# Five edits to the setup of a gated cross-attention kernel: mem read in rows of 128 features, four staging buffers, x transposed earlier, gate's bias added by DMAs

## The chip, the cores and the metric

The kernel runs on one core of a Trainium2 chip. The metric is the device time of one execution in microseconds (us). Before the change it is 984.94 us, the median of three runs (984.9 to 985.8).

## What is computed

Everything is float32. x is (8, 1024, 1024), the context ("mem") is (8, 64, 512). For each of the 8 batches:

```python
mp   = mem @ W_mem.T                      # (64, 1024)
attn = softmax(x @ mp.T / 32)             # (1024, 64)
ctx  = attn @ mp                          # (1024, 1024)
gate = sigmoid(concat(x, ctx) @ W_gate.T + b_gate)
f    = x + gate * ctx
out  = f / sqrt(mean(f*f) + 1e-6) * norm_w
```

The kernel doesn't form ctx before it goes into gate. Since a row of attn adds up to 1, ctx @ W2.T + b_gate is attn @ (mp @ W2.T + b_gate), where W2 is the half of W_gate that meets ctx. So the setup computes mp and "mg" = mp @ W2.T (+ b_gate) once for all 512 rows of mem, and stores both in device memory (`mpd`, mp transposed; `mgd[0]`, mp; `mgd[1]`, mg). The main loop loads 64 rows of each per batch into one tile `mg`: mp in partitions 0 to 63 and mg in partitions 64 to 127.

## The kernel before

**The setup.** mem is loaded as two tiles `memq` (128 rows by 2 by 512), TensorE transposes it in 16 pieces of 128 by 128 (`transpose_mem`, L189), and VectorE and ScalarE copy the pieces from PSUM to `memT`. `chunks` (L107) picks the features of chunk k as every fourth float of a row; w_mem is loaded to match, with four neighbouring rows in one partition (`rows_by_chunk`, L103). Then 32 products `pm` give mp transposed (L213), copied to four tiles `mpT` (m11 to m22). mg is one Strassen step (Winograd's form): seven products `pg` in the order 1, 6, 5, 2, 7, 4, 3 (`mg_product`, L435), summed into c11, c12, c21, c22 by VectorE (`mg_sum`, L450), with gate's bias added by GpSimd (`mg_bias`, L454), and stored to `mgd[1]` (`store_mg`, L459). `store_mp` (L413) has VectorE transpose a quarter of mp into a staging tile `mpq` and stores it to `mgd[0]` by four DMAs; the staging tiles are two buffers, named `it2` and `it3`.

**The main loop.** x comes in 16 parts q of 512 rows, two per batch. x @ W1.T is a two-level Strassen product: seven outer products per q, in the order 1, 6, 7, 5, 4, 2, 3 (`ORDER`, L537), each of seven inner products A, B, C, D, A, E, F (`outer_product`, L683). An inner product is a "slot"; a q has 49. `plan` (L540) puts the other engines' work of a q at slots by hand: `inner_s` (GpSimd, the sums `l` of the left side), `outer_s`, the scores `psT` (slot 7), softmax, the transposed attention `attnT`, the context products `pc` (in outer products 5, 4, 2, 3), `transpose_x` of the next q and so on. The right side's sums are made once: `outer_sum` (L224, tiles t5, t6, t4) and `inner_sum` (L227, tiles it1 to it7, four sums of 128 by 512 for each outer product). Those of 1 are made on VectorE and of 7 and 6 on GpSimd in the setup; those of 5, 4, 2, 3 are spread by L575 over slots 3 to 23 of q=0, on VectorE.

**What sets the order.** `pin` keeps each engine's instructions in the order in which the program writes them, so each engine and each DMA queue is a list worked off from the front; an instruction that waits holds up what stands behind it on its engine. The tile framework adds the waits. Three kinds matter here. A tile with a tag takes a buffer of that tag's pool and waits until its last user is done: `mp_l`, c21 and the `l` tiles share the two buffers of tag `l2`; x of the first q takes the buffer of w_mem (tag `xq`). Plain DMAs all go out on SP's queue (`load`, L97), and each takes the next of eight lanes, so it waits for the DMA eight places ahead of it. The accumulating DMA of the residual (L600) goes out on GpSimd's queue.

**The order around the change** (L465 to L524): sums s1, s2, t7; s3 and the sums of 7 on GpSimd; product 1; store_mp(2), (3); product 6; store_mp(0); product 5 with c12's bias; store_mp(1); t6; load_mp(0); product 2 with c11's bias; w2's sums and t4; GpSimd's sums of 6; product 7; x's transposes and l of product 1; product 4 with c21's bias; x's other transposes; product 3; load_mg(0); then the main loop.

Of the kernel before, what the change touches and what calls it, by code (L numbers as in the profile page):

```python
# [8 lines left out]
F32 = mybir.dt.float32  # L9
AF = mybir.ActivationFunctionType  # L10
ALU = mybir.AluOpType
# [4 lines left out]
P = 128  # L16
# [4 lines left out]
def tile_gated_cross_attention_rmsnorm(  # L21
# [72 lines left out]
    def tt(eng, o, a, b, op):  # L94
        pin(eng.tensor_tensor(o, a, b, op))  # L95

    def load(o, i):  # L97
        pin(nc.sync.dma_start(o, i))

    def t4k(pool, shape, tag, name):  # L100
        return pool.tile(shape, F32, tag=tag, name=name)

    def rows_by_chunk(w, n):  # L103

        return w.rearrange("(p j) f -> p j f", j=n)

    def chunks(t, n):  # L107

        return t.rearrange("p s e -> p (s e)").rearrange("p (m j) -> p j m", j=n)
# [14 lines left out]
    memr = mem.rearrange("b m e -> (b m) e").rearrange("(g s p) e -> g p s e", g=2, p=P)  # L124
    memq = [t4k(rot, [P, 2, E], "l2", f"memq{i}") for i in range(2)]
    wm = t4k(xqpool, [P, KE, D], "xq", "wm")
    wmr = rows_by_chunk(w_mem_t, KE)
    pin(nc.scalar.dma_start(wm[:, 0, :], wmr[:, 0, :]))
    for g in range(2):
        load(memq[g], memr[g])  # L130
# [11 lines left out]
    w1 = [const.tile([P, 4, D], F32, name=f"w1_{h}") for h in range(2)]  # L142
    for h in range(2):
        load(w1[h], rows_by_chunk(w_gate_t[:D, :], KD)[:, 4 * h : 4 * h + 4, :])
    bias_sb = t4k(small, [P, D], "junk", "bias_sb")
    load(bias_sb, b_gate.partition_broadcast(P))
    nw_sb = const.tile([P, D], F32, name="nw_sb")
    load(nw_sb, norm_w.partition_broadcast(P))
    xq = {}
# [1 line left out]
    def load_xq(q):  # L151
        b, n0 = q // QPB, (q % QPB) * QT
        xq[q] = t4k(xqpool, [P, 16, Q4], "xq", f"xq{q}")
        src = x[b, n0 : n0 + QT, :].rearrange("(s c) (i e) -> i c s e", c=32, i=4)
        for i in range(4):
            load(xq[q][32 * i : 32 * (i + 1), :, :], src[i])
# [32 lines left out]
    def transpose_mem(g):  # L189

        cols = slice(g * (BM // 2), (g + 1) * (BM // 2))
        for k in range(KE):
            for r in range(2):
                n = 2 * g + r
                pin(
                    nc.tensor.transpose(
                        pt[k][:, n * P : (n + 1) * P],
                        chunks(memq[g][:, r : r + 1, :], KE)[:, k],
                        ident,
                    )  # L200
                )
            o = memT[k // 2][:, k % 2, cols]
            pin((nc.scalar.copy if k % 2 else nc.vector.tensor_copy)(o, pt[k][:, cols]))
# [23 lines left out]
    def inner_sum(eng, o, n):  # L227
        s, a, b = ((T1, R12, R11), (T2, R22, T1), (R12, R22, R12), (T4, R21, T2))[n]
        tt(eng, w_op(o, s), w_op(o, a), w_op(o, b), ALU.subtract)
# [13 lines left out]
    def transpose_x(q, t, half):  # L243

        key = q, t // 2, half
        if key not in A:
            A[key] = t4k(
                apool, [P, KH, 2 * P], f"a{t // 2 + 1}{half + 1}", f"a{t // 2 + 1}{half + 1}_{q}"
            )
        r = t % 2  # L250
        pin(
            nc.vector.transpose(  # L252
                A[key][:, :, r * P : (r + 1) * P],
                chunks(xq[q][:, 4 * t : 4 * t + 4, :], KD)[:, half * KH : (half + 1) * KH],
            )
        )
# [30 lines left out]
    def inner_s(q, o, part):  # L287
        l11, l12, l21, l22 = quarters(left(q, o))
        if part == 0:
            L2[q, o] = t4k(rot, [P, 4, 2, P], "l2", f"l2_{q}_{o}")  # L290
        s1, s2, s3, s4 = (L2[q, o][:, i, :, :] for i in range(4))
        if part == 0:
            tt(nc.gpsimd, s1, l21, l22, ALU.add)
            tt(nc.gpsimd, s2, s1, l11, ALU.subtract)
        else:
            tt(nc.gpsimd, s3, l11, l21, ALU.subtract)
            tt(nc.gpsimd, s4, l12, s2, ALU.subtract)
# [68 lines left out]
    def load_mp(b):  # L366
        mps[b] = t4k(small, [P, KD, M], "mpb", f"mpb{b}")
        load(mps[b], mpd[:, :, b * M : (b + 1) * M])

    def load_mg(b):  # L370
        mgs[b] = t4k(small, [P, D], "mg", f"mg{b}")
        for g in range(2):
            load(mgs[b][g * M : (g + 1) * M, :], mgd[g, b * M : (b + 1) * M, :])

    KH = KD // 2
# [22 lines left out]
        for r, copy in ((0, nc.vector.tensor_copy), (1, nc.scalar.copy)):  # L400
            pin(copy(mpT[r][j // KH][:, j % KH, :], pm[j][:, r * HM : (r + 1) * HM]))
    (m11, m12), (m21, m22) = mpT
    load_xq(0)
    for r in range(2):
        for h in range(2):
            load(mpd[:, h * KH : (h + 1) * KH, r * HM : (r + 1) * HM], mpT[r][h])

    def mp_step(eng, tag, pool, a, b, op):
        t = t4k(pool, [P, KH, HM], tag, f"mp_{tag}")
# [3 lines left out]
    def store_mp(g):  # L413

        r, n = g // 2, g % 2
        mpq = const.tile([P, 4, Q4], F32, tag=f"it{2 + n}", name=f"mpq{g}")
        for h in range(2):
            pin(
                nc.vector.transpose(
                    chunks(mpq, KD)[:, h * KH : (h + 1) * KH],  # L420
                    mpT[r][h][:, :, n * P : (n + 1) * P],
                )
            )
        for i in range(4):
            load(
                mgd[0, g * P : (g + 1) * P, i * Q4 : (i + 1) * Q4].rearrange(
                    "(s c) e -> c s e", c=32
                ),
                mpq[32 * i : 32 * (i + 1), :, :],
            )  # L430
# [4 lines left out]
    def mg_product(n, l, r):  # L435
        nonlocal mg_next
        pgs = []
        for t in range(2):
            tag = mg_banks[mg_next % 8]
            mg_next += 1  # L440
            pg = (ps_ctx if tag == "ctx" else ps).tile([P, H], F32, tag=tag, name=f"pg{n}_{t}")
            for k in range(KH):
                mm(pg, l[:, k, t * P : (t + 1) * P], r[k], k == 0, k == KH - 1)
            pgs.append(pg)
        return pgs
# [5 lines left out]
        for t in range(2):  # L451
            tt(nc.vector, o[:, t, :], a[:, t, :], pgs[t], ALU.add)

    def mg_bias(eng, o, h):  # L454
        b = bias_sb[:, h * H : (h + 1) * H]
        for t in range(2):
            tt(eng, o[:, t, :], o[:, t, :], b, ALU.add)

    def store_mg(o, r, h):  # L459
        load(  # L460
            mgd[1, r * HM : (r + 1) * HM, h * H : (h + 1) * H].rearrange("(t p) e -> p t e", p=P),
# [14 lines left out]
    pgs = mg_product(1, m11, b11)  # L476
    for t in range(2):
        pin(nc.scalar.copy(c11[:, t, :], pgs[t]))
    store_mp(2)
    store_mp(3)  # L480
    pgs = mg_product(6, s2, t2)
    mg_sum(c21, c11, pgs)
    store_mp(0)
    tt(nc.gpsimd, s2, m12, s2, ALU.subtract)
    pgs = mg_product(5, s1, t1)
    mg_sum(c12, c21, pgs)
    mg_bias(nc.gpsimd, c12, 1)
    store_mp(1)
    w1_place(6)
    outer_sum(6, 3, 5)  # L490
    load_mp(0)
    pgs = mg_product(2, m12, b21)
    mg_sum(c11, c11, pgs)
    mg_bias(nc.gpsimd, c11, 0)
    store_mg(c11, 0, 0)
    w2_sum(nc.vector, b21, b21, t2)
    w1_place(4)
    outer_sum(4, 2, 6)
    for n in range(4):
        inner_sum(nc.gpsimd, 6, n)  # L500
    pgs = mg_product(7, s3, b12)
    mg_sum(c22, c12, pgs)
    mg_sum(c21, c21, pgs)
    store_mg(c22, 1, 1)
    for t in range(2):
        transpose_x(0, t, 0)
    for part in range(2):
        inner_s(0, 1, part)
    for t in (2, 3):
        transpose_x(0, t, 0)  # L510
    pgs = mg_product(4, m22, b21)
    mg_sum(c21, c21, pgs)
    mg_bias(nc.gpsimd, c21, 0)
    store_mg(c21, 1, 0)
    for t in (2, 3):
        transpose_x(0, t, 1)
    outer_s(0, 1)
    for t in range(2):
        transpose_x(0, t, 1)
    pgs = mg_product(3, s2, b22)  # L520
    mg_sum(c12, c12, pgs)
    store_mg(c12, 0, 1)
# [17 lines left out]
    def plan(q):  # L540
        t0 = SLOTS * q
        nxt = q + 1 < NQ
        order = [o for o, _ in ORDER]
        for i, o in enumerate(order):
            for part, t in ((0, 1), (1, 5)):
                if i + 1 < len(order):
                    at(t0 + 7 * i + t, inner_s, q, order[i + 1], part)
                elif nxt:
                    at(t0 + 7 * i + t, inner_s, q + 1, order[0], part)
        at(t0 + 7, scores, q)  # L550
        at(t0 + 7, outer_s, q, 3)
        at(t0 + 7, outer_s, q, 4)
        at(t0 + 9, transpose_scores, q)
        at(t0 + 10, softmax_a, q)
        at(t0 + 13, softmax_b, q)
        at(t0 + 18, transpose_attn, q)
        at(t0 + 21, attn_difference, q)
        if not nxt:
            at(t0 + 5, load_last)
            return  # L560
        at(t0 + 2, load_xq, q + 1)
        for t in (2, 3):
            mid((q, 5), transpose_x, q + 1, t, 0)
            mid((q, 2), transpose_x, q + 1, t, 1)
        for i, t, half in ((36, 0, 0), (38, 1, 0), (43, 0, 1), (45, 1, 1)):
            at(t0 + i, transpose_x, q + 1, t, half)
        mid((q, 3), outer_s, q + 1, 1)
        mid((q, 3), outer_s, q + 1, 2)
        if (q + 1) % QPB == 0:
            at(t0 + 10, load_mp, (q + 1) // QPB)  # L570
            at(t0 + 49, load_mg, (q + 1) // QPB)

    for o in (2, 3):
        w1_place(o)
    for i, (o, n) in enumerate((o, n) for o in (5, 4, 2, 3) for n in range(4)):  # L575
        at(
            (3, 4, 5, 6, 10, 11, 12, 13, 14, 15, 17, 18, 19, 20, 22, 23)[i],
            inner_sum,
            nc.vector,
            o,  # L580
            n,
        )
    slot = 0

    def step():
# [274 lines left out]
```

## Time and profile before

| what | value |
|---|---|
| median of three runs | 984.94 us |
| the profiled execution | 986.23 us |
| its span, first to last instruction | 984.4 us |
| mean granted TensorE clock | 0.996 |
| TensorE busy (PE) | 968.4 us, 98% |
| weight loads (PEld) | 771.3 us, 78% |
| VectorE (DVE) | 823.4 us, 84% |
| GpSimd (POOL) | 722.2 us, 73% |
| ScalarE (ACT) | 324.9 us, 33% |
| DMA, mean over the span | 129 GB/s |

How to read the rows. In a timeline a row is: start in us, length, engine, line, operation, out<-in by the program's names, shape, count, and in brackets how long the engine had been idle and what released it. Most arithmetic goes through helpers, so the line is L92 (products) or L95 (sums) and the tile names tell what it is: pt (mem's transposes), pm (mp), pg (mg), kA to kF (inner products), psT (scores), sc and pa (transposes of the scores and of attn), pc (context). The rows for one tile give the least, median and largest duration in ns, the first and last start, and for DMAs the time from issue to landing. In the 40 slices each digit is a busy share in tenths. A matmul's end is modelled, so the distance of two starts says more than a length.

### The profile page before, as it was taken

Reading aid. Unit: us, or ns where it says so; the run is one execution under the profiler, and the core shown is the slowest. Engines: PE = TensorE matmul, PEld = TensorE weight load, DVE = VectorE, ACT = ScalarE, POOL = GpSimd, SP = SyncE. Lnnn points to the kernel's source line nnn. Section 1 sums busy time; section 2 is a strip of 40 time slices with the busy share of each in tenths; the row PEclk is TensorE's granted clock in tenths of the full one; section 3 lists DMA queues with packets and bytes.
Section 4 is the critical chain, followed back from the end, with each engine's and each line's share of the span. In section 5 each row is a group of like instructions: output and inputs, shape, how many; then the busy total and the mean of one; then the engine's idle time right before and its main releaser. Section 6 shows DMA issues by size and latency. Waiting matters only on the chain.

```text
span 984.4 us, 14254 instructions
## 1 busy us (share of the span) xinstructions
PE 968.4 (98%) x4938; PEld 771.3 (78%) x4938; DVE 823.4 (84%) x1495; ACT 324.9 (33%) x602; POOL 722.2 (73%) x871
## 2 busy tenths in 40 slices
PE   9999999999999999999999999999999999999995
PEld 6546788888887888888887888888888888888873
DVE  3769987979798897979797988979797988979787
ACT  1100225152342424152343434152333334151434
POOL 2345887868787887868787887868787878868772
PEclk9999999999999999999999999999999999999998
DMA  9764346381927355381917364381918374472612
GB/s 368 226 206 120 52 87 139 83 193 46 182 86 137 115 127 126 87 193 48 197 67 145 113 131 116 91 188 57 190 65 158 99 141 106 106 173 67 169 65 86
DMA packets 70631, 126.75 MB, mean 129 GB/s; under 512 B 12320, under 2 KB 49184, under 8 KB 70176
## 3 DMA queue, kind: packets, MB, share of 16 engines
q1 hardware_dynamic: 61776, 93.86, 34.9%
q0 software_dynamic: 8640, 31.46, 17.1%
q8 instruction: 39, 0.64, 0.3%
q10 hardware_dynamic: 144, 0.52, 0.2%
q14 instruction: 32, 0.26, 0.1%
HBM read 85.98 MB, written 39.85 MB: 128 GB/s over the span
## 4 chain that ended last, share of the span: by engine, by line
PE 95%; DVE 2%; POOL 1%; DMA 1%; issue 0%; ACT 0%; DVEq 0%; ACTq 0%
PE kA L92 19%; PE pc L92 11%; PE kE L92 11%; PE kD L92 10%; PE kC L92 10%; PE kF L92 10%; PE kB L92 9%; PE psT L92 6%; PE pg L92 5%; PE pm L92 3%; DVE gate L95 1%; POOL gate L95 1%; DMA memq<-in_mem 1%; DVE gate L674 0%; DVE u L95 0%
## 5 line engine op out<-in xcount | busy, mean ns | idle before, releaser
L95 POOL TENSOR_TENSOR gate<-gate,u 128x256 f32<-128x256 f32 x336 | 271.2, 838 | 123.3 <-DVE u L95 121.3
L596 ACT ACTIVATE gate<-gate 128x512 f32<-128x512 f32 x128 | 79.0, 629 | 403.5 <-DVE gate L95 403.4
L95 POOL TENSOR_TENSOR l<-a 128x256 f32<-128x256 f32 x128 | 129.1, 1009 | 59.7 <-DVE a L95 57.8
L252 DVE STREAM_TRANSPOSE a<-xq 128x512 f32<-128x512 f32 x128 | 137.8, 1098 | 0.0
L92 PE MATMUL pc<-mg,attnT 64*128 64x256 f32 x512 | 127.4, 389 | 0.0
L625 DVE SCALAR_TENSOR_TENSOR gate<-gate,ss,nw_sb 128x512 f32<-128x512 f32 x120 | 124.8, 1049 | 1.1
L92 PE MATMUL kB<-it,l 128*128 128x256 f32 x448 | 115.2, 379 | 0.9 <-DVE gate L95 0.9
L92 PE MATMUL kD<-it,l 128*128 128x256 f32 x448 | 115.0, 379 | 0.0
L92 PEld LDWEIGHTS pc<-mg,attnT 64*128 64x128 f32 x512 | 90.6, 186 | 29.7 <-issue 21.2
L92 PE MATMUL kA<-w,a 128*128 128x256 f32 x384 | 98.7, 379 | 0.4 <-ACT u L740 0.4
L92 PEld LDWEIGHTS kB<-it,l 128*128 128x128 f32 x448 | 85.0, 190 | 13.0 <-DVE gate L95 1.5
L92 PEld LDWEIGHTS kD<-it,l 128*128 128x128 f32 x448 | 85.1, 190 | 11.6
L95 DVE TENSOR_TENSOR gate<-gate,pc 128x512 f32<-128x512 f32 x128 | 86.9, 679 | 5.8 <-ACT gate L596 5.8
L95 POOL TENSOR_TENSOR l<-s 128x256 f32<-128x256 f32 x96 | 76.5, 796 | 7.1 <-DVE s L95 5.5
L92 PEld LDWEIGHTS kA<-w,a 128*128 128x128 f32 x384 | 71.6, 190 | 10.2 <-ACT u L740 0.8
L740 ACT COPY u<-kA 128x256 f32<-128x256 f32 x112 | 40.5, 362 | 102.9 <-PE kA L92 101.8
L92 PE MATMUL kE<-it,a 128*128 128x256 f32 x256 | 69.0, 392 | 0.0
L95 DVE TENSOR_TENSOR u<-u,kB 128x256 f32<-128x256 f32 x112 | 45.4, 405 | 27.7 <-PE kB L92 24.2
L92 PE MATMUL kA<-t,s 128*128 128x256 f32 x256 | 67.4, 386 | 0.0
L92 PE MATMUL kF<-w,l 128*128 128x256 f32 x256 | 65.8, 379 | 0.1
L92 PE MATMUL kC<-w,l 128*128 128x256 f32 x256 | 65.7, 379 | 0.0
L610 ACT ACTIVATE junk<-gate 128x1024 f32<-128x1024 f32 x60 | 63.5, 1058 | 1.6 <-DMA gate<-in_x 0.7
(126 smaller groups left out, 1994.3 us busy)
## 6 DMA issues: line engine op xcount, KB each, us to landing
xq<-in_x SPq DMA_DIRECT2D x64, 512.0 KB, 9.2
gate<-in_x POOLq DMA_DIRECT2D x60, 512.0 KB, 7.8
out<-gate SPq DMA_DIRECT2D x60, 512.0 KB, 2.6
w<-in_w_gate_t SPq DMA_DIRECT2D x8, 512.0 KB, 11.2
w<-in_w_gate_t SPq DMA_DIRECT2D x2, 2048.0 KB, 15.6
mg<-mgd SPq DMA_DIRECT2D x16, 256.0 KB, 3.7
mpd<-mpT SPq DMA_DIRECT2D x4, 512.0 KB, 11.7
mgd<-mpq SPq DMA_DIRECT2D x16, 128.0 KB, 2.6
```

Source lines behind the costliest of these rows:

```text
L92: pin(nc.tensor.matmul(o, lhsT, rhs, start=start, stop=stop, skip_group_check=True))
L95: pin(eng.tensor_tensor(o, a, b, op))
L252: nc.vector.transpose(A[key][:, :, r * P : (r + 1) * P], chunks(xq[q][:, 4 * t : 4 * t + 4, :], KD)[:, half * KH : (half + 1) * KH],)
L596: pin(nc.scalar.activation(g, g, AF.Sigmoid))
L610: nc.scalar.activation(junk, O[q, t], AF.Square, accum_out=ss[:, t % 2 : t % 2 + 1])
L625: nc.vector.scalar_tensor_tensor(g[:, cols], g[:, cols], rstd[:, t % 2 : t % 2 + 1], nw_sb[:, cols], ALU.mult, ALU.mult,)
L740: pin(nc.scalar.copy(p1, kb["A"]))
```

## The change

1. The features of mem's chunk k are now the 128 neighbouring ones from 128k on, so the transposes read rows of adjacent floats; w_mem is loaded to match (`(k p) d -> p k d`).
2. `load_xq(0)` now stands behind the four stores of mpT to `mpd`.
3. The four quarters of mp have a staging tile each (`it4`, `it6`, `it2`, `it3` for g = 0 to 3), and all four `store_mp` and `load_mp(0)` stand together after product 1.
4. x's transposes of half 0 and l of product 1 (`inner_s(0, 1, ...)`) move from after product 7 to after product 6; the half-1 transposes of t = 0, 1 to before product 7.
5. The bias tile, its load and `mg_bias` go. Instead `add_bias` adds b_gate to partitions 64 to 127 of each batch's `mg` tile by an accumulating DMA on GpSimd's queue, at slot 8 of each even q.
6. The sums of 5, 6 and 4 are all made by GpSimd in the setup (5 after t6; 6 and 4 after t4); slots 3 to 6 and 10 to 13 of q=0 keep those of 2 and 3 on VectorE.

```diff
-    wmr = rows_by_chunk(w_mem_t, KE)
+    wmr = w_mem_t.rearrange("(k p) d -> p k d", p=P)
...
-    bias_sb = t4k(small, [P, D], "junk", "bias_sb")
-    load(bias_sb, b_gate.partition_broadcast(P))
...
-                        pt[k][:, n * P : (n + 1) * P],
-                        chunks(memq[g][:, r : r + 1, :], KE)[:, k],
-                        ident,
+                        pt[k][:, n * P : (n + 1) * P], memq[g][:, r, k * P : (k + 1) * P], ident
...
+    def add_bias(b):
+        pin(nc.gpsimd.dma_start(mgs[b][M:P, :], b_gate.partition_broadcast(M), accum_op=ALU.add))
...
-    load_xq(0)
     for r in range(2):
         for h in range(2):
             load(mpd[:, h * KH : (h + 1) * KH, r * HM : (r + 1) * HM], mpT[r][h])
+    load_xq(0)
...
-        mpq = const.tile([P, 4, Q4], F32, tag=f"it{2 + n}", name=f"mpq{g}")
+        mpq = const.tile([P, 4, Q4], F32, tag=f"it{(4, 6, 2, 3)[g]}", name=f"mpq{g}")
...
-    store_mp(2)
-    store_mp(3)
+    for g in (2, 3, 0, 1):
+        store_mp(g)
+    load_mp(0)
     pgs = mg_product(6, s2, t2)
     mg_sum(c21, c11, pgs)
-    store_mp(0)
     tt(nc.gpsimd, s2, m12, s2, ALU.subtract)
+    for t in range(4):
+        transpose_x(0, t, 0)
+    for part in range(2):
+        inner_s(0, 1, part)
     pgs = mg_product(5, s1, t1)
     mg_sum(c12, c21, pgs)
-    mg_bias(nc.gpsimd, c12, 1)
-    store_mp(1)
     w1_place(6)
     outer_sum(6, 3, 5)
-    load_mp(0)
+    for n in range(4):
+        inner_sum(nc.gpsimd, 5, n)
     pgs = mg_product(2, m12, b21)
     mg_sum(c11, c11, pgs)
-    mg_bias(nc.gpsimd, c11, 0)
     store_mg(c11, 0, 0)
     w2_sum(nc.vector, b21, b21, t2)
     w1_place(4)
     outer_sum(4, 2, 6)
-    for n in range(4):
-        inner_sum(nc.gpsimd, 6, n)
+    for o in (6, 4):
+        for n in range(4):
+            inner_sum(nc.gpsimd, o, n)
+    for t in range(2):
+        transpose_x(0, t, 1)
     pgs = mg_product(7, s3, b12)
...
-    for t in range(2):
-        transpose_x(0, t, 0)
-    for part in range(2):
-        inner_s(0, 1, part)
-    for t in (2, 3):
-        transpose_x(0, t, 0)
     pgs = mg_product(4, m22, b21)
     mg_sum(c21, c21, pgs)
-    mg_bias(nc.gpsimd, c21, 0)
...
-    for t in range(2):
-        transpose_x(0, t, 1)
...
+        if q % QPB == 0:
+            at(t0 + 8, add_bias, q // QPB)
...
-    for i, (o, n) in enumerate((o, n) for o in (5, 4, 2, 3) for n in range(4)):
-        at(
-            (3, 4, 5, 6, 10, 11, 12, 13, 14, 15, 17, 18, 19, 20, 22, 23)[i],
-            inner_sum,
-            nc.vector,
-            o,
-            n,
-        )
+    for i, (o, n) in enumerate((o, n) for o in (2, 3) for n in range(4)):
+        at((3, 4, 5, 6, 10, 11, 12, 13)[i], inner_sum, nc.vector, o, n)
```

More of the change, by code (lines that the diff above doesn't have):

```diff
@@ L452, in mg_sum @@
             tt(nc.vector, o[:, t, :], a[:, t, :], pgs[t], ALU.add)
-    def mg_bias(eng, o, h):
-        b = bias_sb[:, h * H : (h + 1) * H]
-        for t in range(2):
-            tt(eng, o[:, t, :], o[:, t, :], b, ALU.add)
     def store_mg(o, r, h):
@@ L517, in tile_gated_cross_attention_rmsnorm @@
     outer_s(0, 1)
-    for t in range(2):
-        transpose_x(0, t, 1)
     pgs = mg_product(3, s2, b22)
```

## The prediction

> **What bounds the kernel now.** I read the busy table first, then the order of TensorE's work in time, then the waits in the one stretch where that order has holes, and last what VectorE and GpSimd do there.
>
> ```profile
> PE   9999999999999999999999999999999999999995
> PE 95%; DVE 2%; POOL 1%; DMA 1%; issue 0%; ACT 0%; DVEq 0%; ACTq 0%
> ```
>
> TensorE is busy in every slice, and the chain that ended last is 95% TensorE. So only two things shorten this kernel: TensorE doing some work faster, or closing a hole in its stream. The timeline of the setup and of the scores' starts shows where either is possible:
>
> ```profile
> 6.66 3.66 PE L196 MATMUL pt<-ident,memq 128*128 128x128 f32 x16 [0.83 <-DMA memq<-in_mem]
> 10.11 27.97 PE L92 MATMUL pm<-memT,wm 128*128 128x512 f32 x64
> 79.12 7.03 PE L92 MATMUL pg<-w,mp_s 128*128 128x512 f32 x16
> ...
> 92.12 3.67 PE L92 MATMUL psT<-a,mpb 128*64 128x256 f32 x32
> 150.53 2.81 PE L92 MATMUL psT<-a,mpb 128*64 128x256 f32 x24
> 205.58 1.73 PE L92 MATMUL psT<-a,mpb 128*64 128x256 f32 x14
> ```
>
> From 10.11 to 92.12 each row starts where the row before it ends: the setup's engines other than TensorE are already hidden. The scores start once per q (512 rows of x), so the distance of two starts is one q: 150.53 - 92.12 = 58.41 us for q=0, 205.58 - 150.53 = 55.05 for q=1, and all later ones are 55.04 to 55.05. **q=0 loses 3.37 us**, and no other q loses anything. Inside it:
>
> ```profile
> 105.79 0.41 PE L346 MATMUL pa<-ident,e 128*128 128x128 f32 x2
> 107.98 1.10 PE L92 MATMUL kF<-w,l 128*128 128x256 f32 x4
> 110.82 1.13 PE L92 MATMUL kB<-it,l 128*128 128x256 f32 x4 [0.87 <-DVE gate L95]
> 112.55 0.70 PE L92 MATMUL kC<-t,l 128*128 128x256 f32 x2 [0.61 <-POOL l L95]
> 106.00:120.00 14.00, 12.47 (x61) 9.61 (x60) 13.83 (x25) 3.12 (x6) 10.75 (x13) 1.00 0.01 1
> ```
>
> Set against the same instructions of q=1, offset from their scores' start, pa is 0.25 us late, kF adds 0.2, kB 1.0, kC 0.9, and the rest of the 3.37 comes up to offset 27. The last row (columns: stretch, length, PE, PEld, DVE, ACT, POOL busy) says why: VectorE is busy 13.83 of 14.00 us. It carries 16 inner sums (L575-582) in q=0 alone, 8 of them in slots 14 to 23.
>
> **What the Trainium skill says.** (1) "SBUF — State Buffer", section "Door 1: The DMA port swizzle (why `[64,N]` ≈ `[32,N]`)": SBUF is read in lines of 16 bytes, and each access that crosses to a new line pays. mem's transposes take every fourth float, 16 bytes apart. The weight loads agree:
>
> ```profile
> L196 PEld LDWEIGHTS pt<-ident,memq x16: 195/231/231, 6.6 to 9.7; 128*128 128x128 f32 x16
> L320 PEld LDWEIGHTS sc<-ident,sT x32: 140/141/143, 97.3 to 926.6; 128*128 128x128 f32 x32
> ```
>
> 231 ns strided, 141 ns where the 128 floats are adjacent. (2) The same page, "Who interferes with whom": a VectorE instruction with two SBUF inputs contends with a GpSimd instruction that reads SBUF. The trace agrees: GpSimd's 128x512 sums take 1.28 us beside transposes or PSUM sums (76.00) and 1.71 us beside VectorE's w2 sums (68.37). (3) "DMA: Bandwidth & Descriptors", "SWDGE vs HWDGE vs iDMA": an accumulating DMA is issued from GpSimd only. Agrees: the residual's, at L600, sit on GpSimd's queue.
>
> **1. mem's chunks (L127, L198).** The trace starts 16 strided transposes in 10.11 - 6.66 = 3.45 us, 0.215 each; the two sc transposes at 97.56 are followed by the next product at 97.78, 0.11 each. If only that counted, 16 x 0.105 = 1.7 us. But memq's second half is issued at 1.2 and lands 6.6 us later (its landing row's maximum), at 7.8. So: first eight 6.66 to 7.55; wait until about 7.95; second eight to 8.85; pm starts at about 8.9 behind the last copy (0.42 each). Gain 10.11 - 8.9 = **1.2 us**. Bounds: 0, if the spacing were set by something else than the stride, and 1.7. w_mem's rows keep 4 KB or more each; the third and fourth chunk land at 2.3 + 9.4 = 11.7 and are first used 13.7 us after 8.9: nothing. Who can't follow 1.2 us earlier? VectorE's sums of w1 end at 31.6, pm's first copy would be due at 30.9; the copies take 0.43 and come every 0.86, so 0.7 us is caught up within two.
>
> **2. mpd's stores ahead of x's loads on SP's queue (L403-406).** The four stores (512 KB) now issue from 33.9 to 38.3, x's four (512 KB) at 38.8 to 40.2 instead of 38.1 to 39.6. Now all eight have landed by 40.14 + 11.7 = 52 at the latest. x is first read at 51.7 (step 4); VectorE then has some 4 us to spare before it waits for TensorE again at 64.1. Cost 0.
>
> **3. Four staging buffers (L416, L476).** All eight transposes to mpq now stand in a row: 8 x 1.02 = 8.1 us, 42.3 to 50.4. The 4.87 us that VectorE waited for the stores of the first pair goes, but TensorE never waited for it. c21's sums of product 6 come at 50.4 to 51.7 instead of 48.5 to 52.6; their banks are next used by product 4, near 71. The 16 stores and mpb's load leave SP about 9 us earlier. it4 and it6 lend their buffers, so GpSimd's sums of 6 and 4 wait for stores that land near 57, and run after 79. Cost 0.
>
> **4. x's first transposes and l of product 1 in the middle.** VectorE: four transposes at 51.7 to 55.9, in place of the wait above; two more before product 7's sums. By my count of its rows it ends s2 of q=0 at about 86.7, where shifted by 1.2 it would be 88.7. GpSimd is the dear place. l of product 1 takes the buffer that mp_l holds until product 7 has read it, so it waits until 72.4 - 1.2 = 71.2, and queued behind it are 12 inner sums (5, 6, 4), then l of product 6, which in turn takes product 1's buffer and waits for its last matmul, near 90.9. Sum: 71.2 + 4 x 0.74 + 12 x 1.28 = 89.5: just in time. l's first half, two adds of 0.73 to 1.18, is ready by 93.3; kB of product 6 is due at 96.69 - 1.2 = 95.5. Margin 2.2 us; at 1.71 a sum, 12 x 0.43 = 5.2 us more, it is lost. VectorE's rows there are mostly PSUM sums and transposes, so I take 1.28 to 1.45.
>
> **5. gate's bias.** Removed: six GpSimd adds (2.51 + 2.95 + 2.52 = 8.0 us, off TensorE's path) and one 512 KB load. Added: eight accumulating DMAs of 256 KB, one per two q, at slot 8. An issue on GpSimd takes 0.87 us and 0.2 beside it, bounded by what this row's idle time covers:
>
> ```profile
> L600 POOL DMA_DIRECT2D gate<-in_x x60: 829/868/1178, 135.1 to 918.5; - x60
> DMA to landing us min/median/max: 5.0/7.8/14.5
> 213.03 2.54 POOL L95 TENSOR_TENSOR gate<-gate,u 128x256 f32<-128x256 f32 x3 [1.71 <-DVE u L95]
> ```
>
> GpSimd idles 1.71 us exactly there: hidden. In q=0 the idle time is 0.55 us, and 0.5 us of delay meets a product that needs it 0.9 us later: hidden. The issue waits for mg's load, and the gate sums and l's second half are queued behind it on GpSimd; in q=2 that load is issued at 197.75 and lands within 4.3 us, slot 8 is at 210. Landing: issue at offset 5.8, needed by the first context product at offset 20.6, so 14.8 us; residuals of twice the size took 5.0 to 14.5. I take 0; above, 0.5 us in one or two of the eight. A gain is excluded, since nothing here is on TensorE's path now.
>
> **6. VectorE in q=0.** Eight inner sums leave it (0.7 to 0.9 us each, 6.4 us), all of slots 14 to 23. Slots 3 to 6 and 10 to 13 keep four each, so the late softmax (pa, 0.25 to 0.28 us) stays; after it VectorE holds what it holds in every later q. Gain 3.37 - 0.28 = **3.1 us**. Bounds 1.0 and 3.37.
>
> **Sum.** -1.2 - 3.1 = -4.3 us. The profiled execution took 986.23 us, span 984.4; it would become 981.9, span 980.1. The runs' median lies 1.29 below that execution, at 984.94; the same step gives **980.6 us**, 0.44% less.
>
> **Rivals.**
> - GpSimd's twelve sums run contended (step 4): 71.2 + 4.4 + 20.4 = 96.0, l's first half at 98.2, product 6 stalls 2.8 us, its successors little more. Gain 1.3: 983.6. For: one order, no idle time. Against: the rates at 76.00. 10%.
> - q=0's stall moves instead of going, to GpSimd's l (it ended one hole, 0.61) or to VectorE's gate sums: half of 3.1 returns: 982.2. 10%.
> - The transposes are paced by something else than the stride: 981.8. 10%.
> - Slower: the accumulating DMA lands after the context product wants it. It decides from 14.8 us on, and each us beyond costs 8 us in all. At 16.0: 8 x 1.2 = 9.6, less 4.3: 990.2. Against: half a residual's bytes. 4%.
>
> **How the numbers follow.** My forecast has 66%, own range 979.8 to 981.6. With the second and third rival the range is 979.7 to 982.4, about 8 in 10. A measurement here tells about 0.2%, 2 us, from no change. Faster by more (below 983.0): the forecast, the third rival and most of the second: 87%. Within: the first rival mostly, 9%. Slower: 4%.
>
> **What would show it.** Right: pm starts near 8.9; the distance of the first two scores' starts is 55.3 or so; GpSimd's last sum of 4 ends before 92. Wrong: pm still at 10.1; kB or kC of product 6 with idle time behind GpSimd's l; context products waiting for a DMA in even q.

## The result, and the profile after

| | before | after |
|---|---|---|
| median, run beside each other on one chip | 985.4 us (984.9 to 986.14, 6 runs) | 982.46 us (982.29 to 982.67, 6 runs) |
| ratio, 95% interval | | 0.997 (0.9957 to 0.9982) |
| the profiled execution, its span | 986.23, 984.4 us | 982.54, 980.7 us |

The changed kernel is faster by about 2.6 us (985.03, the median of 33 runs of before, less 982.46), where 4.3 was forecast: right in sign, but 982.46 is 1.86 us above the forecast 980.6, and 0.06 us above the upper end of the range. Further runs of before fall into two groups: two thirds or more at 984.8 to 985.1 us, the others at 985.9 to 986.3 (half of the six in the table, so their median is too high). The profiled execution of before (986.23) is one of the longer ones, which matters below; so a second profile, of an execution of 984.97 us (e12), stands in the middle column here. All values are differences of starts in the timelines, in us:

| | before, profiled | before, e12 | after |
|---|---|---|---|
| start of the first transpose of mem | 6.66 | 6.67 | 5.82 |
| from there to the first pm | 3.45 | 2.39 | 2.39 |
| first pm to q=0's scores | 82.01 | 81.85 | 81.90 |
| q=0 (its scores to the next q's) | 58.41 | 58.40 | 56.95 |
| the rest of the span | 833.87 | 833.89 | 833.64 |
| span | 984.4 | 983.2 | 980.7 |

Against e12 the span falls by 2.5: 0.85 at the first transpose, 1.45 in q=0, 0.25 after the last scores (917.71 after, 919.96 in e12), nothing from the first transpose to pm. The 3.7 between the two profiled executions hold 1.2 more, 1.06 of it between the first transpose and pm, which is the difference of two executions and not of two kernels.

The page of the changed kernel, the chain that ended last by engine:

```profile
PE 93%; POOL 3%; DVE 2%; issue 1%; ACT 0%; DVEq 0%; POOLq 0%; ACTq 0%
```

TensorE's share of the chain fell from 95% to 93%, and GpSimd's rose from 1% to 3%. That looks odd in a faster kernel: a new stretch of the chain, from 70.4 to 103.6 us, runs over GpSimd. TensorE's timeline, changed kernel, shows where it comes back:

```profile
5.82 2.53 PE L194 MATMUL pt<-ident,memq 128*128 128x128 f32 x16
8.21 5.97 PE L92 MATMUL pm<-memT,wm 128*128 128x512 f32 x13
...
90.11 3.67 PE L92 MATMUL psT<-a,mpb 128*64 128x256 f32 x32
103.60 1.13 PE L92 MATMUL kC<-w,l 128*128 128x256 f32 x4 [1.37 <-POOL l L95]
147.06 3.67 PE L92 MATMUL psT<-a,mpb 128*64 128x256 f32 x32
202.10 3.67 PE L92 MATMUL psT<-a,mpb 128*64 128x256 f32 x32
```

The holes of before, from 105.79 on behind VectorE and GpSimd, are gone: no later instruction of q=0 waits. In their place stands one hole, at kC of product 7, for GpSimd's sum l. Set against q=1 by offset from the scores, kB of product 7 is 0.16 late, kC 1.63 and kD 0.11: 1.90 of the 1.91 in 56.95 - 55.04. What GpSimd did up to then, changed kernel:

```profile
70.49 0.73 POOL L95 TENSOR_TENSOR l<-a 128x256 f32<-128x256 f32 x1 [18.25 <-PE pg L92]
...
80.97 2.25 POOL L95 TENSOR_TENSOR t<-t 128x512 f32<-128x512 f32 x1
...
84.41 1.27 POOL L95 TENSOR_TENSOR it<-t 128x512 f32<-128x512 f32 x1
85.76 2.14 POOL L95 TENSOR_TENSOR it<-t,it 128x512 f32<-128x512 f32 x1
...
89.53 1.73 POOL L95 TENSOR_TENSOR it<-t,it 128x512 f32<-128x512 f32 x1
...
93.49 1.71 POOL L95 TENSOR_TENSOR l<-s 128x256 f32<-128x256 f32 x1
...
98.64 0.98 POOL L372 DMA_DIRECT2D mg<-in_b_gate  x1
99.37 3.05 POOL L95 TENSOR_TENSOR gate<-gate,u 128x256 f32<-128x256 f32 x3
102.38 1.17 POOL L95 TENSOR_TENSOR l<-a 128x256 f32<-128x256 f32 x1
```

This is a list without a gap from 70.49 to past 105. Ahead of it GpSimd sat idle for 18.25 us, until product 7 had read the buffer that l of product 1 takes. Then come l of product 1, the twelve inner sums (73.36 to 91.22, 17.86 us, 1.49 each), l of product 6 (four adds, 5.6 us in all), l of product 7's first adds, the bias DMA's issue, three gate sums, and only then the adds that kC waits for. The sums cost 1.27 where nothing disturbs them, 2.25 once at 80.97 and 1.72 to 2.14 for the last three; there VectorE does s (from 80.05 and from 84.78) and the sums of 2, as its timeline shows, changed kernel:

```profile
84.78 1.98 DVE L95 TENSOR_TENSOR s<-s,a 128x1024 f32<-128x1024 f32 x1
88.70 1.43 DVE L95 TENSOR_TENSOR it<-w,it 128x512 f32<-128x512 f32 x1
```

The eight accumulating DMAs of the bias, and their landing (changed kernel, by tile):

```profile
L372 POOL DMA_DIRECT2D mg<-in_b_gate x8: 826/826/977, 98.6 to 868.9; - x8
DMA to landing us min/median/max: 4.9/7.1/7.7
```

No context product waits for one.

### The profile page after: what moved, and what is told of

The parts are those of the page before. It is cut to its first block, busy times and chain, and to the rows that moved or that the text cites. A ratio compares the mean times of both kernels' runs of the same rounds, so it can differ in the third digit from the quotient of the medians.

```text
span 980.7 us, 14277 instructions
## 1 busy us (share of the span) xinstructions
PE 965.9 (98%) x4938; PEld 770.1 (79%) x4938; DVE 819.0 (84%) x1487; ACT 324.9 (33%) x602; POOL 730.5 (74%) x881
## 4 chain that ended last, share of the span: by engine, by line
PE 93%; POOL 3%; DVE 2%; issue 1%; ACT 0%; DVEq 0%; POOLq 0%; ACTq 0%
PE kA L92 19%; PE pc L92 12%; PE kE L92 11%; PE kF L92 10%; PE kD L92 10%; PE kC L92 9%; PE kB L92 9%; PE psT L92 6%; PE pg L92 4%; PE pm L92 3%; POOL it L95 1%; DVE gate L95 1%; POOL l L95 1%; POOL gate L95 1%; PE pz L92 0%
```

## Experiments on q=0's hole

My theory: GpSimd's list is too long by about 1.6 us when product 7 wants its l, through two parts: contention with VectorE's two-input sums, and the bias issue. The rival: the hole is VectorE's, moved (its late u and gate sums). A further question is whether the eight sums that left VectorE were the cause of the old stall at all. Medians are compared with 985.03 us of before (984.96 beside e5, e6, e8, e9; 984.97 beside e7, e10); each ratio is to before.

**e1: the bias issue of q=0 eight slots later.**

```diff
-            at(t0 + 8, add_bias, q // QPB)
+            at(t0 + (8 if q else 16), add_bias, q // QPB)
```

> The changed kernel, with the bias DMA of q=0 at slot 16 instead of slot 8 (other q unchanged). Forecast of the prediction (the issue is hidden): q=0 stays 56.95 us long and the wait of kC in product 7 stays 1.37 us. Theory A (GpSimd has no gap from 70.5 to 105 us, so every instruction put in that list before l's second half of product 7 is paid by TensorE in full): that half comes about 0.7 us earlier, the distance from the bias issue's start to the next gate sum, so q=0 takes about 56.2 us and the kernel 0.7 us less than the changed one. Theory B (what delays l is VectorE's sums of 3 in slots 10 to 13, which read two SBUF operands beside it): at most 0.3 us less.

Measured 981.59 us (981.48 to 981.85), ratio 0.9963 (0.995 to 0.9975); q=0 takes 56.12. kC of product 7 is 0.58 late, no longer 1.63. GpSimd's timeline, e1:

```profile
98.69 2.55 POOL L95 TENSOR_TENSOR gate<-gate,u 128x256 f32<-128x256 f32 x3
101.20 1.18 POOL L95 TENSOR_TENSOR l<-a 128x256 f32<-128x256 f32 x1
```

The gate sums start where the issue stood; l starts 1.18 earlier, 0.68 from the issue and 0.50 from shorter gate sums. So the issue costs 0.83 us in q=0 (56.95 - 56.12).

**e9: no bias DMAs at all** (after, without the eight; b_gate is left out of the output).

```diff
-        if q % QPB == 0:
-            at(t0 + 8, add_bias, q // QPB)
```

> The changed kernel without gate's bias: the eight accumulating DMAs are left out, so b_gate is not in the output. If only the one in q=0 costs time: as with that one moved to slot 16, 981.6 us, all other q at 55.04 to 55.05 as they are. If the other seven cost something that the scores' starts don't show, or the one at slot 16 still costs: below 981.4.

Measured 981.51 us (981.36 to 981.78), ratio 0.9961 (0.9948 to 0.9974); q=0 56.10, every later q 55.04 to 55.05. That is e1 within 0.1 us: the other seven DMAs cost nothing, and only the issue in q=0 is paid.

**e2: the sums of 3 later**, out of the slots that the softmax uses.

```diff
-        at((3, 4, 5, 6, 10, 11, 12, 13)[i], inner_sum, nc.vector, o, n)
+        at((3, 4, 5, 6, 17, 18, 19, 20)[i], inner_sum, nc.vector, o, n)
```

> The changed kernel, with the four sums of 3 on VectorE at slots 17 to 20 instead of 10 to 13. Theory A (the length of GpSimd's list alone): GpSimd's instructions keep their lengths, kC of product 7 still waits 1.2 to 1.4 us, q=0 stays near 56.9. Theory B (contention): the three gate sums of product 6 shrink from 3.05 us to some 2.2 and l of product 7 from 1.17 to 0.73, so the wait falls by about 1.2 us and q=0 takes about 55.6 us. Either way pa is no longer late by 0.25 us. Rival to both: the sums at 17 to 20 make a new hole there, q=0 57 us or more.

Measured 981.57 us (981.52 to 981.92), ratio 0.9963 (0.995 to 0.9975); q=0 56.16. GpSimd's three gate sums fall from 3.05 to 2.37 us and l starts at 101.23; kC of product 7 is 0.30 late. But 0.61 comes back at kC of product 5, near 109, in the stretch to which the sums went: TensorE has 0.44 us of idle time behind GpSimd's l there, with VectorE busy for all of 106 to 110. GpSimd's list isn't full there: it waits 0.68 us for VectorE's u, and then its gate sums take 2.93 us where they took 2.09 in the changed kernel, e2:

```profile
105.13 2.93 POOL L95 TENSOR_TENSOR gate<-gate,u 128x256 f32<-128x256 f32 x3 [0.68 <-DVE u L95]
```

So at slots 17 to 20 a crowded VectorE (the rival) seems to have its part in the new hole, beside the contention; no run separates the two. The result lies between the two theories.

**e10: the sums of 2 later**, away from GpSimd's sums of 4.

```diff
-        at((3, 4, 5, 6, 10, 11, 12, 13)[i], inner_sum, nc.vector, o, n)
+        at((21, 22, 23, 24, 10, 11, 12, 13)[i], inner_sum, nc.vector, o, n)
```

> The changed kernel with the four sums of 2 on VectorE at slots 21 to 24 instead of 3 to 6, where they stood beside GpSimd's sums of 4 and l of product 6. If it is the contention that filled GpSimd's list: from 85.8 to 96.8 us GpSimd's rows there took 1.72 to 2.14 us for a 128x512 sum instead of 1.27 and 1.06 to 1.71 for an l instead of 0.73, 4.5 us in all; s2 and the outer sums still stand there, so some 2.5 us of it goes, l of product 6 starts near 90.1, and kC of product 7 waits less than 0.2 us: q=0 about 55.4 us, the kernel 981.0. If the list is too long in any case (12 sums at 1.27 behind a start at 70.5): the wait shrinks by half a us at most, 982.0. Rival: new holes beside the context products in slots 21 to 24, q=0 57 us or more.

Measured 981.74 us (981.56 to 981.96), ratio 0.9964 (0.995 to 0.9978); q=0 55.97. GpSimd's timeline, e10:

```profile
87.68 1.27 POOL L95 TENSOR_TENSOR t<-t 128x512 f32<-128x512 f32 x1
88.91 1.26 POOL L95 TENSOR_TENSOR it<-t,it 128x512 f32<-128x512 f32 x1
```

With VectorE's sums of 2 gone, the last two sums of 4 fall from 1.72 and 1.73 to 1.27 and 1.26. kC of product 7 waits no more. The time expected wasn't reached: kE of product 5 and kC of product 4, with the kD behind it, now lose 0.65 between them, and pa is 0.23 late. The trace names no releaser; VectorE, which has the four sums in slots 21 to 24, is busy for 7.97 of the 8 us from 110 to 118.

**e3: the sums of 5 ahead of l of product 1**, so that GpSimd uses the 18 us in which it waits for a buffer.

```diff
-    for part in range(2):
-        inner_s(0, 1, part)
     pgs = mg_product(5, s1, t1)
...
         inner_sum(nc.gpsimd, 5, n)
+    for part in range(2):
+        inner_s(0, 1, part)
```

> The changed kernel, with the four sums of 5 ahead of l of product 1 in GpSimd's list, where it stood idle for 18 us until product 7 had read the buffer. Theory A: the work behind is 5 us less, GpSimd's last sum of 4 ends near 86, l of product 6 starts when product 1's last matmul releases its buffer (90.0) instead of 91.2, and kC of product 7 waits about 0.2 us instead of 1.37: q=0 about 55.8 us, the kernel 1.1 us less than the changed one. Theory B (contention in slots 8 to 13) and a third theory, that the wait comes from the late sum a21 on VectorE: no change in q=0, 56.95 us.

Measured 980.76 us (980.71 to 980.87), ratio 0.9954 (0.994 to 0.9968); q=0 55.38, where only pa is late, by 0.30. GpSimd's timeline, e3:

```profile
83.01 1.27 POOL L95 TENSOR_TENSOR it<-t,it 128x512 f32<-128x512 f32 x1
90.08 0.92 POOL L95 TENSOR_TENSOR l<-s 128x256 f32<-128x256 f32 x1 [5.80 <-PE kF L92]
...
100.09 0.73 POOL L95 TENSOR_TENSOR l<-a 128x256 f32<-128x256 f32 x1
```

The last sum of 4 ends 7 us earlier, at 84.28; GpSimd then idles for 5.80 us, and the l that kC waits for starts at 100.09. It gained 1.7, more than the 1.1 expected. The order of the list is enough to close the whole hole, the bias issue included: with slack ahead of it, the same issue at the same slot delays no product. VectorE's list is the same as in the changed kernel, so this hole was not VectorE's, moved: that rival is out.

**e6: e1, e2 and e3 together** (the three diffs above).

> The changed kernel with the three moves together: bias DMA of q=0 at slot 16, sums of 3 at slots 17 to 20, sums of 5 ahead of l of product 1. Theory A and B in part each: the hole at kC is gone with GpSimd's five us, and pa's 0.30 us goes with the sums of 3, so q=0 takes 55.05 to 55.15 us like every other and the kernel 980.4 us, the least of all. Rival: the hole of 0.61 at kC of product 5, which the kernel with only the sums of 3 moved showed, stays: 55.7 us and 981.0.

Measured 980.38 us (980.36 to 980.71), ratio 0.9952 (0.9939 to 0.9964). q=0 takes 55.04, what every other q takes: nothing is late. It is the fastest of all versions, 2.1 us below the changed kernel.

**e5: before, with its eight sums of 2 and 3 spread out.** Nothing goes to GpSimd.

```diff
-            (3, 4, 5, 6, 10, 11, 12, 13, 14, 15, 17, 18, 19, 20, 22, 23)[i],
+            (3, 4, 5, 6, 10, 11, 12, 13, 18, 21, 24, 27, 29, 32, 35, 36)[i],
```

> The kernel before, with all its 16 inner sums still on VectorE in q=0, but those of 2 and 3 at slots 18, 21, 24, 27, 29, 32, 35, 36 instead of 14 to 23. If it is the crowding of VectorE in slots 14 to 23 that cost q=0 its 3.37 us (step 6 of the prediction): only pa's 0.25 us and little more stays, q=0 about 55.5 us and the time 2.8 us less than before, 982.2. If it is the amount of VectorE's extra work in q=0, wherever it stands: new holes beside the context products in slots 21 to 36, q=0 57 us or more, 983.7 or more.

Measured 982.62 us (982.57 to 983.55), ratio 0.9975 (0.9965 to 0.9986), q=0 56.03, between the two expectations. Eight indices alone bring 2.34 us: the place of these sums in slots 14 to 23 was the cause of most of the old stall, and GpSimd's help wasn't needed for that. Besides pa's 0.25, 0.59 us is now lost at kE of product 2 (130.74), four slots behind the last of the sums.

**e8: two staging buffers in the changed kernel.**

```diff
-        mpq = const.tile([P, 4, Q4], F32, tag=f"it{(4, 6, 2, 3)[g]}", name=f"mpq{g}")
+        mpq = const.tile([P, 4, Q4], F32, tag=f"it{2 + n}", name=f"mpq{g}")
```

> The changed kernel with two staging buffers for mp's rows (it2 and it3) instead of four, all four transposes still in a row. VectorE then waits for the first stores in the middle of the row, some 3 to 5 us. If the four buffers are worth nothing to TensorE, as step 3 says, because VectorE waits 4 us for x right behind them anyway: time as the changed one within 0.3 us, 982.5. Rival: sums of product 6 and x's transposes come so late that product 4 waits for w2's sums or the first slots for l: 983.5 or more.

Measured 986.36 us (985.2 to 987.45), ratio 1.0015 (1.0008 to 1.0021): 3.9 us slower than the changed kernel, where the same time was expected; the rival came true. VectorE's timeline, e8:

```profile
55.54 3.90 DVE L418 STREAM_TRANSPOSE mpq<-mpT 128x512 f32<-128x512 f32 x4 [10.12 <-DMA mgd<-mpq]
```

The third and fourth quarter wait 10.12 us for the stores of the first two. x's transposes, c21's sums and t4 stand behind them; the sums of w2 and t4 now run beside l of product 1 (1.66 and 2.66 us for two adds that take 0.73 in after); l of product 6 starts at 94.81 instead of 91.22, and kB of product 6 stands idle for 3.47 us. q=0 takes 60.47, 5.43 more than every other q, and the wait accounts for 3.63 of it. The rest comes behind it. TensorE, a stretch (columns as in the prediction, behind the five engines the granted clock, the DMA share and GB/s) and the transposes sc in it, e8:

```profile
98.24 1.42 PE L92 MATMUL kB<-it,l 128*128 128x256 f32 x4 [3.47 <-POOL l L95]
99.00:102.00 3.00, 3.00 (x9) 2.35 (x8) 0.59 (x2) 0.00 (x0) 2.88 (x4) 0.50 0.66 107
L316 PEld LDWEIGHTS sc<-ident,sT x2: 231/231/231, 99.0 to 99.5; 128*128 128x128 f32 x2
L316 PE MATMUL sc<-ident,sT x2: 421/421/421, 99.5 to 99.7; 128*128 128x128 f32 x2
```

From about 98.9 to 102.3 TensorE had half its clock: a product of 128x256 took 634 ns instead of 379, a transpose of 128x128 421 instead of 273, its weight load 231 instead of 140. That costs another 1.8 us. The four buffers bring no time of their own, but the new order can't be had without them.

## Experiments on mem's transposes

**e4: edit 1 alone**, on the kernel before.

```diff
-    wmr = rows_by_chunk(w_mem_t, KE)
+    wmr = w_mem_t.rearrange("(k p) d -> p k d", p=P)
...
-                        pt[k][:, n * P : (n + 1) * P],
-                        chunks(memq[g][:, r : r + 1, :], KE)[:, k],
-                        ident,
+                        pt[k][:, n * P : (n + 1) * P], memq[g][:, r, k * P : (k + 1) * P], ident
```

> The kernel before, with only the first edit (mem's chunks of 128 adjacent features, w_mem to match). If the stride sets the pace of the 16 transposes: from the first transpose to the first product of mp 2.3 to 2.4 us instead of 3.45, q=0 unchanged at 58.41, span and time 1.1 us less than before. Rival: the earlier start is lost in a later wait of the setup (mp's copies behind VectorE's sums of w1, product 6 behind s2), time unchanged; or the first transpose starts earlier because of the new w_mem load, and the gain is 1.9 us as in the profile of the changed kernel.

Measured 984.14 us (984.01 to 984.39), ratio 0.9989 (0.9983 to 0.9996): 0.89 gained. But the way in which it came wasn't the one expected: the first transpose starts at 5.71, pm at 8.19. In e5, whose setup is that of before, the *strided* transposes went from 6.76 to 9.11, in 2.35 us: no slower than the adjacent ones. Two runs settle it.

**e12: the kernel before once more.** No edit.

> The kernel before once more, unchanged, for the profile of one more of its executions: the profiled one (986.23 us) had its 16 transposes 0.215 us apart, while most executions take 985.0. Theory A: the stride sets the pace of the transposes always, so that pm starts 3.4 us after the first transpose in this one too, and the 1.2 us between executions lies elsewhere. Theory B: in an execution of 985.0 us the first transpose starts near 6.7 as before, and pm 2.35 to 2.5 us later, near 9.1; the pace of 3.45 us belongs to the longer executions alone.

Measured 984.97 us (ten runs, 984.84 to 986.25), ratio 0.9998 (0.9989 to 1.0007). TensorE's timeline and the group by tile (duration in ns, least, median, largest), e12:

```profile
6.67 2.55 PE L196 MATMUL pt<-ident,memq 128*128 128x128 f32 x16 [1.01 <-DMA memq<-in_mem]
9.06 3.35 PE L92 MATMUL pm<-memT,wm 128*128 128x512 f32 x7
```

```profile
L196 PE MATMUL pt<-ident,memq x16: 285/286/357, 6.7 to 8.9; 128*128 128x128 f32 x16
```

In the profiled execution of before the same 16 took 421 ns each. That is the time of a transpose at half clock in e8, and so is its weight load of 231 ns; both were measured there on adjacent rows. The rows of the changed kernel's transposes, and of the warm-up products pz that open before's profiled execution:

```profile
L194 PE MATMUL pt<-ident,memq x16: 272/273/447, 5.8 to 8.1; 128*128 128x128 f32 x16
L92 PE MATMUL pz<-zeros x10: 634/634/793, 1.2 to 5.2; 128*128 128x256 f32 x10
```

pz takes 634 ns, as products of its shape did in e8 at half clock. In the changed kernel the first three transposes take 421 to 447 ns and most of the others 273, with adjacent rows; in e12 all are quick, with strided ones. So TensorE begins an execution at half pace and goes over to the full one: at about 5.3 us in e12, at 6.5 in the changed kernel, and in the profiled execution of before only near 10.4, behind all 16 transposes. (The view of the granted clock shows 1.00 over this whole stretch in each of the three, so this is read from the durations.) The pace of 0.215 us from which step 1 was worked out is TensorE's half pace in that execution, not the price of the stride. At full pace the stride shows in the weight loads (213 ns against 142 after) and a little in the distance of two starts (0.122 us in e12 against 0.109 after), some 0.2 us for 16; that both take 2.39 us from the first transpose to pm is in part chance, since the changed kernel had its first transposes at half pace and e12 none.

**e11: before, with w_mem's rows in a row, and mem's transposes still strided.**

```diff
-    wmr = rows_by_chunk(w_mem_t, KE)
+    wmr = w_mem_t.rearrange("(k p) d -> p k d", p=P)
```

> The kernel before, with only the first half of edit 1: w_mem's four loads of 128 rows take the rows in a row (0 to 127, 128 to 255, ...) instead of every fourth row; mem's transposes stay at the stride of 16 bytes. Left out: the match of mem's features with w_mem's rows, so the product is of permuted features. Why: the setup of the kernel before ran a second time in e5, and there the 16 strided transposes took 2.35 us (6.76 to 9.11), no longer than the adjacent ones of e4 (5.71 to 8.19, 2.48); what differs is the first start, 6.76 against 5.71, with the four loads at the start landing 0.8 to 1.1 us earlier in e4. Theory A (what step 1 said: the stride of the transposes costs, the loads are the same): no gain, about 985.0, first transpose near 6.7. Theory B (the order of w_mem's rows lets the first loads, mem's among them, land earlier, and the stride costs little): first transpose at 5.7 to 5.8, pm at 8.0 to 8.3, and 984.0 to 984.2, nearly all of e4's gain. If the stride's slow pace (3.45 us) shows in some executions only, those are about 1 us longer in both.

Measured 984.13 us (984.07 to 984.28), ratio 0.9988 (0.9981 to 0.9994): all of e4's gain, with strided transposes. mem's loads and the landing time, by tile, e11:

```profile
L98 SPq DMA_DIRECT2D memq<-in_mem x2: 434/453/472, 0.7 to 1.2; - x2
...
DMA to landing us min/median/max: 4.9/5.3/5.8
```

They land 0.9 us earlier than in e12 (5.8/6.2/6.6), issued at the same moment. mem's own load is the same instruction in both; what differs is w_mem's three loads. The first is in flight beside mem's on ScalarE's queue (landing 4.2 instead of 5.1 us) and now reads 128 neighbouring rows instead of every fourth. The other two can't be the cause: in both traces none of their packets starts before 6.2 us, and the DMA engines fall behind earlier, between 4 and 5 us (last columns: DMA share, GB/s), first e12, then e11:

```profile
4.00:5.00 1.00, 1.00 (x4) 0.82 (x3) 0.00 (x0) 0.00 (x0) 0.00 (x0) 1.00 0.78 244
4.00:5.00 1.00, 1.00 (x4) 0.82 (x3) 0.00 (x0) 0.00 (x0) 0.00 (x0) 1.00 1.05 406
```

The gain of edit 1 is in a DMA, not in TensorE. Why every fourth row is slower isn't shown.

**e7: before, with edit 1 and e5's spread**, nothing else of the change.

> The kernel before with two edits alone: mem's chunks of 128 adjacent features, and the sums of 2 and 3 spread over slots 18 to 36. If the two gains add up as each alone gave them (0.89 and 2.34 us): 981.75 us, less than the changed kernel's 982.46, so that the other edits (staging buffers, the order in the middle, the bias by DMAs, twelve sums on GpSimd) gave nothing that this needs. If they share a part (a later start of q=0 hides some of the crowding): 982.5 or more.

Measured 981.75 us (981.73 to 982.11), ratio 0.9964 (0.9952 to 0.9977); q=0 56.06. The gains of e4 and e5 add up (0.89 + 2.34 = 3.23; 3.22 measured). Two small edits give 0.7 us more than the whole change does as it stands.

## Why the prediction was right and wrong

- **Steps 4 and 5 failed, in q=0.** Step 4 took the twelve sums at 1.28 to 1.45 us, found a margin of 2.2 us at kB of product 6, put no cost into the sum, and followed GpSimd's list no further. The sums took 1.49 each, and at product 6 a margin was left: the first half of l was ready at 93.5, kB started at 94.69. But l of product 6 took 5.6 us for its four adds, so that the list reached l of product 7 late, and that product waited. The contention that I had seen in the trace of before (1.71 beside VectorE's w2 sums), and that the Trainium skill states ("SBUF — State Buffer", "Who interferes with whom"), came with VectorE's s and the sums of 2; I had reckoned with transposes and PSUM sums there. e10 shows it: without the sums of 2 beside it, l of product 7 starts 2.3 us earlier and kC doesn't wait. Step 5 covered the issue in q=0 with idle time (0.55 us) read off the trace of before, from a list that the change itself lengthens by eight sums. In the changed list that idle time doesn't exist, and e1 measures the price, 0.83 us. The sign that I named for this was also too narrow: the last sum of 4 ended at 91.2, "before 92", and product 6 didn't wait. It fell one product later. Rival 2 described where it went, and its 982.2 is nearest; the cause was rival 1's, contended sums.
- **Step 6 was right in its cause, and its gain was spent by step 4.** VectorE's stall did go (e5 shows the cause of most of it; its last 0.5 us stood at offset 29 to 30, at kC of product 4 behind GpSimd's l, and not by 27 as I read). Of 3.1 us, 1.45 were left (58.40 to 56.95). e3 and e6 return the rest: 55.38 and 55.04. The remainder I left at pa is there, 0.30 in e3, and goes only when the sums of 3 leave slots 10 to 13 (e6).
- **Step 1 was near in size (1.2 forecast, 0.85 in the spans, 0.89 alone) and wrong in mechanism.** I read TensorE's half pace in one execution as the price of the stride, and supported it with a weight load of 231 ns, which is what adjacent weights take at half clock (e8). In the changed kernel some adjacent loads reach 230 too, and in e12 strided ones take 213. The third rival's premise, that something else paces the transposes, was true; the 0.89 us came from elsewhere. I had also put w_mem's loads at nothing; its first load is where the gain is. The Trainium skill's lines of 16 bytes ("SBUF — State Buffer", "Door 1: The DMA port swizzle (why `[64,N]` ≈ `[32,N]`)") fit the longer weight loads, 213 against 142 ns, but a longer weight load isn't a later product.
- **Step 2, cost 0: right**, by less than I thought. x was to have landed by 52, but its last load went out at 42.0, took up to 12.5 us, and x's transposes started at 54.63 after 4.03 us of idle time. (The trace puts that wait down to a store of mpq, which is the last event it saw; 42.0 + 12.5 = 54.5 points to x.) The 4 us of VectorE's slack that step 2 named took it up.
- **Step 3, cost 0: right for the changed kernel**, but the reason, that TensorE never waited for these buffers, holds for the old order alone; e8 shows that the new order needs them.
- **Step 5's other seven DMAs, cost 0: right** (e9), landing in 4.9 to 7.7 us against the 14.8 allowed.
- **The sum.** Missing: 1.65 (step 6's gain spent) and 0.35 (step 1). Gained besides: 0.25 after the last scores, whose cause stays open. That is 1.75 of the 1.86 between 980.6 and 982.46.

**Still open:** what sets the moment at which TensorE goes over to its full pace. In the 13 other profiles it lies between about 4.5 and 7.1 us, in the profiled execution of before near 10.4. That this is what makes some executions of before about 1 us longer is shown in one profile only; in e11's series 11 of 33 runs of before were longer, and none of the 42 runs of e4 and e11. Those two start their transposes with little or no idle time behind the warm-up products, before sits idle for 0.8 to 1.0 us; that this keeps the pace low was not tried. e8, which has edit 1, also has longer runs (7 of 20, by about 1 us, with a mean granted clock of 0.993 against 0.994 to 0.996), and none of them was profiled.

## What to carry to other kernels

Before work is moved to an engine that has room on average, write down that engine's list from the instruction that holds it up to the next one that somebody waits for, at contended durations, and put work that depends on nothing ahead of the instruction that waits for a buffer: e3 is a move of two lines and gave 1.7 us. Follow the list past the first wait that it just meets. Idle time read off a trace is cover only for edits that leave that list as it is. A pace read from a single execution is no property of an instruction until a second execution, or another row with the same operation, shows it too, at the same clock.

## What the runs showed of the hardware

- The order of rows in one DMA's source moved the landing of another DMA: with w_mem's first 128 rows adjacent instead of every fourth (each row 4 KB), that load landed in 4.2 instead of 5.1 us and mem's, in flight beside it, in 5.3 instead of 6.2 (e11 against e12).
- After 3.47 us without work TensorE ran at half the granted clock from about 98.9 to 102.3 us (e8), and the wait cost 5.4 us instead of 3.6. Holes of up to 1.37 us (changed kernel) left the products behind them at 379 ns. At the start of each execution TensorE ran at half pace, 634 ns for 128x256, for some us, while the view of the clock showed 1.00.
- GpSimd's sums beside VectorE's sums from two tiles in SBUF: 128x512 from 1.27 to between 1.72 and 2.25 us, 128x256 from 0.73 to 1.71; VectorE's own 128x512 sums in the same stretch 0.9 to 1.43 (changed kernel).
- The issue of the bias's accumulating DMA occupied GpSimd for 0.83 to 0.98 us; in q=0 the next instruction started 0.73 to 0.75 us after the issue began (changed kernel, e1, e3).
